# A two-layer block on one core: the first loads on two queues, the first LayerNorm in pairs of tiles, one weight product moved to the second batch, GpSimd's splits moved to VectorE, and W2's preparation tied to gates

## The chip, the cores and the metric

The kernel runs on one core of a Trainium2 chip. Its time is device time in microseconds, from runs of the whole program; the median of three runs is the number that counts. The profile is one execution of the same program, read by the hardware profiler, and its times are counted from the first instruction (the span's start).

## The reference

The input is x of shape (4, 512, 256): four batches of 512 tokens with 256 features. Two layers are applied. Because the state of the first layer's recurrence starts at zero and only one step is taken, the recurrence is a product with one fixed matrix. With `ln` for LayerNorm without scale, and `H` for the Walsh-Hadamard transform over 1024 values:

```
layer 0:  n  = ln(x)
          s  = n + rmsnorm(n @ M) * norm_w        M = W_in.T * diag(g) * W_out.T
layer 0 gate:  x = x + s * silu(ffn(n))           ffn(n) = H(silu(n @ W1.T) * (n @ W3.T)) @ W2.T
layer 1:  n  = ln(x)
          s  = n + causal_attention(ln(n) * gamma + beta)
layer 1 gate:  x = x + s * silu(ffn(n))           with the second layer's W1, W2, W3
output x
```

In the kernel the attention's query and key weights are multiplied once to one matrix (wqk), and its value and output weights to another (wvo). H is symmetric, so the kernel applies it to W2 once, and not to the hidden values. All values are float32; the kernel splits each operand into a high and a low part of 12 bits (hi + lo), so that a float32 product is three passes of TensorE: hi*hi, hi*lo, lo*hi.

## The kernel before

**Phases.** The work is eight phases in a row: four batches in layer 0, then four in layer 1. The body of a phase is one feed-forward block, `ffn` (L310), of a whole batch. It goes over eight chunks of 128 hidden values. For each chunk TensorE computes two banks of up products (`f_0gu` for batch 0 of layer 0: one bank with W1, one with W3; 6 products of 512 columns each, L70). ScalarE takes silu of the first bank (L363), VectorE multiplies it with the second (L364, the gate product), and `split` (L59) makes hi and lo: a copy on ScalarE (L61) and a subtraction (L62). Then TensorE adds the chunk's down products (`f_0dn`, L332). The banks `gu` are three, so every third bank waits for the silu or the gate product that frees it.

**Beside.** All other work (LayerNorm, mixer, attention, weight preparation) is written as generators. `Beside` spreads their steps over the 16 slots of a feed-forward block. A scheduler of the language then decides the order of each engine's queue; `tc.issue_after` (through `after`, L307) forces one instruction behind another.

**The first phase.** Batch 0 of layer 0 is special, for the weights must be prepared in it. `ffn` gets `parts=2` (chunk 0 in two halves of the tokens), `NH` as `defer` (all down products stay until the end), and `behind=True`, which puts the slots behind the gate products. In front of it stands the start:

- SP issues all loads, in the order: four tiles of x, the identity, qk, W13's part 0, vo, W13's part 1, the two halves of W2, the Hadamard matrix, bc, W_out, W_in, W13's parts 2 and 3, and small ones.
- Seven products of zeros (`warm`, L582) keep TensorE busy while the loads are under way.
- `norm_first` (L263) takes each of the four token tiles on its own: statistics and sum on VectorE, the power on GpSimd (L238), normalisation on VectorE (L240), two transposes on TensorE (L273), and the split of the transposed tile into `xth` (ScalarE) and `xtl` (VectorE).
- `prep_qk` computes wqk from the query and key weights, `prep_vo` computes wvo, and three butterfly stages of W2's first half (L125, L126) follow.
- `split_w13` (L97) splits W13's four parts, each 128x1024, when `ffn` first needs them. Parts 2 and 3 of layer 0 have their subtraction on GpSimd:

```python
engine = nc.gpsimd if layer == 0 and q >= 2 else nc.vector
```

- `prep_w2` (L113) transforms W2 by three butterfly stages on VectorE and a product with the Hadamard matrix on TensorE (`w2ps`; the first half in float32, the second in two passes after a split).
- `prep_m` (L178) makes M: a few small VectorE operations, four scalings on ScalarE (`wg`), and a product on TensorE (`mps`).

Of the kernel before, what the change touches and what calls it, by code (L numbers as in the profile page):

```python
# [21 lines left out]
P = 128  # L22
D = 256
# [12 lines left out]
def kernel(ctx: ExitStack, tc: tile.TileContext, a: dict, out: bass.AP):  # L36
# [22 lines left out]
    def split(src, hi, lo, engine=nc.vector):  # L59
        """hi + lo = src, exactly."""  # L60
        nc.scalar.copy(hi, src)  # L61
        engine.tensor_tensor(lo, src, hi.bitcast(F32), ALU.subtract)  # L62

    def mm3(o, terms):
        """o = sum over terms of lhs.T @ rhs, each operand a pair (hi, lo)."""
        seq = [(l[0], r[0]) for l, r in terms]
        for l, r in terms:
            seq += [(l[0], r[1]), (l[1], r[0])]
        for n, (l, r) in enumerate(seq):
            nc.tensor.matmul(o, l, r, start=n == 0, stop=n == len(seq) - 1)  # L70

# [6 lines left out]
    def load_x(b, nt=NT):  # L78
        xs[b] = x_slot(f"x{b}", [P, NT, D])
        src = a["x"][b].rearrange("(t p) d -> p t d", p=P)  # L80
        for t in range(0, NT, nt):
            nc.sync.dma_start(xs[b][:, t : t + nt, :], src[:, t : t + nt, :])
# [9 lines left out]
    def load_w13(layer, q):  # L92
        raw = t4(f"w13raw_{layer}_{q}", [P, 2, S])
        nc.sync.dma_start(raw, a[f"w13_{layer}"][q])
        return raw

    def split_w13(layer, q, raw):  # L97
        hi = wp.tile([P, 2, S], F32R, tag="w13h", name=f"w13h_{layer}_{q}", bufs=4)
        lo = wp.tile([P, 2, S], F32R, tag="w13l", name=f"w13l_{layer}_{q}", bufs=4)
        for c in range(2) if (layer, q) == (0, 0) else (slice(None),):  # L100
            cs = slice(c * D, (c + 1) * D) if c in (0, 1) else c
            engine = nc.gpsimd if layer == 0 and q >= 2 else nc.vector
            split(raw[:, :, cs], hi[:, :, cs], lo[:, :, cs], engine)
# [9 lines left out]
    def prep_w2(layer, raws, dst, scratch):  # L113
        """Rows of W2 under the Walsh-Hadamard transform (it is symmetric, so it may act on
        W2 in place of the hidden values): over the 8 blocks by butterflies, over the 128
        rows of a block by a product with the +-1/32 matrix."""
        w2h, w2l = dst
        for half in range(2):
# [10 lines left out]
            # in float32 it costs TensorE two passes more, but no split beforehand  # L129
# [23 lines left out]
    def product_of_weights(name, lhsT, rhs, nk, scale=None):  # L153
        """[256, 256] = lhsT.T @ rhs over nk chunks of 128, in float32, as a (hi, lo) pair."""
        hi = wp.tile([P, 2, D], F32R, name=f"{name}h")
        lo = wp.tile([P, 2, D], F32R, name=f"{name}l")
        o = psum(f"{name}ps", [P, 2, D])
        for i in range(2):
# [19 lines left out]
    def prep_m(win, wout):  # L178
        """xi*(sum of C_real*B_real - C_imag*B_imag) between W_in and W_out is one matrix."""
# [16 lines left out]
    def load_pair(name):  # L196
        raw = t4(f"{name}raw", [P, 2, 2, D])
        nc.sync.dma_start(raw, a[name])
        return raw

    def prep_qk(qk):
        return product_of_weights(
            "wqk", lambda k, i: qk[:, 0, k, sl(i)], lambda k: qk[:, 1, k, :], 2, 1.0 / 16.0
        )
# [7 lines left out]
    def moments(name, x, mr):  # L212
        """mr[:, 0] = the tokens' means, mr[:, 1] = their 1 / sqrt(variance + eps)"""
# [10 lines left out]
    def layernorm(name, x, y, groups=(NT,)):  # L224
        """y = layernorm(x), the token tiles in groups of these sizes"""
# [37 lines left out]
    def norm_first():  # L263
        """norm(0, 0), each token tile on its own"""
# [4 lines left out]
        layernorm("ln0_0", xs[0], xn, (1,) * NT)  # L269
        for t in range(NT):  # L270
            o = psum(f"xt0_0tp{t}", [P, 2, P])
            for k in range(2):
                nc.tensor.transpose(o[:, k, :], xn[:, t, sl(k)], ident)  # L273
            split(o, hi[:, :, sl(t)], lo[:, :, sl(t)])

    def norm(layer, b):
# [4 lines left out]
        layernorm(f"ln{layer}_{b}", xs[b], xn)  # L281
        yield
        if layer:
            # The second normalisation acts on the transposed values: its moments as rows of
            # all tokens, in every partition.
# [24 lines left out]
    def ffn(name, xT, w13, w2, slot, defer=1, spare=(), last=None, parts=1, behind=False):  # L310
        """Up, silu gate, down with the transformed W2: two PSUM banks of two token tiles.
        The down products of a chunk follow the up products of the defer-th after it.
        spare: pairs of tiles that hold the split hidden values of the first chunks.
        last: called with each token tile's result, finished one after the other, each in a
        bank of its own."""
# [20 lines left out]
                    # A start clears the accumulate bits of its whole bank: the bank's second  # L336
                    # tile begins without one, behind the first's.
# [10 lines left out]
        for c in range(NH):  # L348
# [7 lines left out]
            for half in range(parts if c == 0 else 1):  # L356
                n = S // (parts if c == 0 else 1)
                ts_ = slice(half * n, (half + 1) * n)
                for o, cols in gu:
                    mm3(o[:, ts_], k_pairs((wh, wl), cols, xT, ts_))  # L360
# [3 lines left out]
            gates.append(nc.vector.tensor_tensor(h, h, gu[1], ALU.mult))  # L364
            if c < len(spare):
# [6 lines left out]
            with after(gates[-1] if behind else None):  # L372
# [386 lines left out]
```

## Time and profile before

| what | value |
|---|---|
| runs | 372.45, 373.54, 375.09 us; median 373.54 us |
| profiled execution | span 370.9 us, 5491 instructions; no other time of it is given |
| TensorE (PE) busy | 361.5 us, 97% of the span |
| VectorE (DVE) busy | 248.0 us, 67% |
| ScalarE (ACT) busy | 179.7 us, 48% |
| GpSimd (POOL) busy | 36.2 us, 10% |
| loads and stores | 15.50 MB in 8969 packets |
| chain that ended last | PE 90%, DVE 5%, DMA 2% |

How to read it: a row of the profile names the line of the kernel, the engine, the operation, and what is written from what is read by the program's own names with buffer numbers left out, so `f_0gu` stands for both banks of all eight chunks in the first layer's first batch (and the second layer's). A busy share is of the whole span. In the slices each digit is the busy share of 1/40 of the span in tenths. "Idle before" names the instruction or load that ended an engine's idle time.

### The profile page before, as it was taken

The page shows a single profiled execution, that of the slowest core. Times are in us where ns is not written, and L with a number is a line of the kernel's source. Part 1 is how long each engine was busy: PE and PEld are TensorE (multiplying, and loading weights), DVE is VectorE, ACT ScalarE, POOL GpSimd, SP SyncE. Part 2 cuts the span into 40 slices and gives each one's busy share as a digit, 9 for nine tenths or more (in the row PEclk, how much of TensorE's full clock was granted, in tenths as well). Part 3 has the DMA queues.
Part 4 walks back from the last instruction along what each step waited for, and adds up shares of the span by engine and source line. Part 5 has one row for each costly group of instructions (what it writes and reads, how often), then busy time and mean ns, then how long its engine had stood idle before and what let it go on. Part 6 is the DMA issues. An engine that isn't in the chain of part 4 may idle for free.

```text
span 370.9 us, 5491 instructions
## 1 busy us (share of the span) xinstructions
PE 361.5 (97%) x2167; PEld 318.2 (86%) x2167; DVE 248.0 (67%) x519; ACT 179.7 (48%) x334; POOL 36.2 (10%) x30
## 2 busy tenths in 40 slices
PE   6997999999999999999999999999999999999995
PEld 4875999888888898889888998988989898888895
DVE  6898948996499339945949487465846447374644
ACT  2765334624453335445553654266633646356451
POOL 2060023410025002400011000010000000000000
PEclk9999999999999999999999999999999999999999
DMA  7915200000000040110010001100003000010001
GB/s 234 389 51 203 80 2 1 2 0 2 0 3 0 0 171 0 58 57 2 1 59 0 0 2 57 59 1 2 0 2 114 2 0 1 2 57 2 1 2 57
DMA packets 8969, 15.50 MB, mean 42 GB/s; under 512 B 848, under 2 KB 6640, under 8 KB 8944
## 3 DMA queue, kind: packets, MB, share of 16 engines
q1 hardware_dynamic: 8944, 15.16, 11.7%
q8 instruction: 17, 0.28, 0.3%
q14 instruction: 8, 0.07, 0.1%
HBM read 13.04 MB, written 2.11 MB: 41 GB/s over the span
## 4 chain that ended last, share of the span: by engine, by line
PE 90%; DVE 5%; DMA 2%; SPq 1%; issue 0%; ACT 0%; DVEq 0%
PE f_3gu L70 12%; PE f_2gu L70 12%; PE f_1gu L70 12%; PE f_0gu L70 8%; PE f_0dn L332 6%; PE f_3dn L332 6%; PE f_1dn L332 6%; PE f_2dn L332 6%; PE sc L70 4%; PE pv L70 4%; PE o L70 3%; PE v L70 3%; PE tq L70 3%; DMA w2raw<-in_w 2%; DVE w2b L125 1%; PE pt L498 1%
## 5 line engine op out<-in xcount | busy, mean ns | idle before, releaser
L70 PE MATMUL f_0gu<-xtl,w13h 128*128 128x512 f32 (+1 forms) x68 | 25.8, 382 | 0.0
L70 PE MATMUL f_1gu<-xth,w13l 128*128 128x512 f32 x64 | 25.5, 399 | 0.0
L70 PE MATMUL f_0gu<-xth,w13l 128*128 128x512 f32 (+1 forms) x68 | 25.5, 384 | 0.0
L70 PE MATMUL f_3gu<-xtl,w13h 128*128 128x512 f32 x64 | 25.5, 398 | 0.0
L70 PE MATMUL f_2gu<-xth,w13l 128*128 128x512 f32 x64 | 25.3, 396 | 0.0
L70 PE MATMUL f_3gu<-xth,w13l 128*128 128x512 f32 x64 | 25.3, 396 | 0.0
L70 PE MATMUL f_1gu<-xtl,w13h 128*128 128x512 f32 x64 | 25.3, 396 | 0.0
L70 PE MATMUL f_2gu<-xtl,w13h 128*128 128x512 f32 x64 | 25.3, 395 | 0.0
L70 PE MATMUL f_0gu<-xth,w13h 128*128 128x512 f32 (+1 forms) x68 | 21.3, 393 | 2.5 <-DVE f_0h L364 2.5
L364 DVE TENSOR_TENSOR f_2h<-f_2h,f_2gu 128x512 f32<-128x512 f32 x16 | 10.9, 681 | 19.1 <-PE f_2gu L70 11.0
L61 ACT CAST f_2hh<-f_2h 128x512 fp32r<-128x512 f32 x16 | 9.9, 621 | 23.0 <-DVE f_2h L364 23.0
L70 PE MATMUL f_2gu<-xth,w13h 128*128 128x512 f32 x64 | 20.7, 397 | 0.0
L70 PE MATMUL f_1gu<-xth,w13h 128*128 128x512 f32 x64 | 20.7, 398 | 0.0
L70 PE MATMUL f_3gu<-xth,w13h 128*128 128x512 f32 x64 | 20.6, 397 | 0.0
L61 ACT CAST f_3hh<-f_3h 128x512 fp32r<-128x512 f32 x16 | 9.9, 620 | 19.7 <-DVE f_3h L364 19.7
L332 PE MATMUL f_3dn<-w2l,f_3hh 128*128 128x256 f32 x64 | 17.6, 281 | 0.0
L332 PE MATMUL f_2dn<-w2l,f_2hh 128*128 128x256 f32 x64 | 17.6, 282 | 0.0
L332 PE MATMUL f_3dn<-w2h,f_3hh 128*128 128x256 f32 x64 | 17.5, 281 | 0.0
L332 PE MATMUL f_2dn<-w2h,f_2hh 128*128 128x256 f32 x64 | 17.5, 281 | 0.0
L332 PE MATMUL f_1dn<-w2l,f_1hh 128*128 128x256 f32 x64 | 17.4, 281 | 0.0
L332 PE MATMUL f_1dn<-w2h,f_1hh 128*128 128x256 f32 x64 | 17.3, 281 | 0.0
L363 ACT ACTIVATE f_2h<-f_2gu 128x512 f32<-128x512 f32 x16 | 9.5, 596 | 16.0 <-PE f_2gu L70 16.0
(227 smaller groups left out, 1104.4 us busy)
## 6 DMA issues: line engine op xcount, KB each, us to landing
w13raw<-in_w SPq DMA_DIRECT2D x8, 512.0 KB, 6.2
w2raw<-in_w SPq DMA_DIRECT2D x4, 512.0 KB, 6.8
mrb<-there SPq DMA_DIRECT2D x4, 512.0 KB, 3.7
x<-in_x SPq DMA_DIRECT2D x3, 512.0 KB, 3.7
out<-x SPq DMA_DIRECT2D x6, 256.0 KB, 2.1
x<-in_x SPq DMA_DIRECT2D x4, 128.0 KB, 2.2
qkraw<-in_qk SPq DMA_DIRECT2D x1, 512.0 KB, 4.7
voraw<-in_vo SPq DMA_DIRECT2D x1, 512.0 KB
```

What stands on the lines that cost most here:

```text
L61: nc.scalar.copy(hi, src)
L70: nc.tensor.matmul(o, l, r, start=n == 0, stop=n == len(seq) - 1)
L125: nc.vector.tensor_tensor(nv[:, :, 0], cv[:, :, 0], cv[:, :, 1], ALU.add)
L332: return nc.tensor.matmul(o, l[:, sl(t)], r[:, c, :], start=start, stop=stop, skip_group_check=True)
L363: nc.scalar.activation(h, gu[0], AF.Silu)
L364: gates.append(nc.vector.tensor_tensor(h, h, gu[1], ALU.mult))
L498: nc.tensor.transpose(pt[:, sl(j)], p[:, sl(j)], ident)
```

## The change

- **Loads.** x's four tiles go out by SP and ScalarE in turns, and qk follows on ScalarE's queue. On SP come the identity, W13's part 0 in two halves, part 1, W2, the Hadamard matrix, parts 2 and 3, and then bc, W_out and W_in. vo is no longer loaded at the start.
- **First LayerNorm.** `norm_first` is a generator: two pairs of tiles, each with one sum and one power, four transposes into one bank, and one split of 512 columns. The product of qk is cut in two (`product_qk`); its first half stands ahead of the first pair's transposes, its second half behind them.
- **Order.** `split_w13` puts the second half of part 0 behind the splits of the transposed x, and later parts behind that. Chunk 0's products go by term (hi*hi of both banks, then hi*lo, then lo*hi). A slot stands behind the gate product and behind the chunk's last up product. LayerNorms of batches 2 and 3 stand behind a gate product.
- **Weights.** W2's preparation runs in the slots, with no step of it in the start; the split of wqk and the load of the next x follow it. wvo is made in the second batch.
- **GpSimd** has no part in the splits of W13 any more.
- There are eight products of zeros instead of seven.

```diff
-            nc.sync.dma_start(xs[b][:, t : t + nt, :], src[:, t : t + nt, :])
+            queue = queues[t // nt % len(queues)]
+            queue.dma_start(xs[b][:, t : t + nt, :], src[:, t : t + nt, :])
...
     def load_w13(layer, q):
         raw = t4(f"w13raw_{layer}_{q}", [P, 2, S])
-        nc.sync.dma_start(raw, a[f"w13_{layer}"][q])
+        n = 2 if (layer, q) == (0, 0) else 1
+        for cs in (slice(i * S // n, (i + 1) * S // n) for i in range(n)):
+            nc.sync.dma_start(raw[:, :, cs], a[f"w13_{layer}"][q][:, :, cs])
...
     def split_w13(layer, q, raw):
...
-        for c in range(2) if (layer, q) == (0, 0) else (slice(None),):
-            cs = slice(c * D, (c + 1) * D) if c in (0, 1) else c
-            engine = nc.gpsimd if layer == 0 and q >= 2 else nc.vector
-            split(raw[:, :, cs], hi[:, :, cs], lo[:, :, cs], engine)
+        if (layer, q) != (0, 0):
+            split(raw, hi, lo)
+            return hi, lo
+        halves = [slice(c * D, (c + 1) * D) for c in range(2)]
+        split(*(z[:, :, halves[0]] for z in (raw, hi, lo)))
+        next(normed)
+        with after(first["norm"][0]), after(first["norm"][1]):
+            hi_, lo_ = split(*(z[:, :, halves[1]] for z in (raw, hi, lo)))
+        first["w13"] = hi_, lo_
...
+    def product_qk(qk):
+        o = psum("wqkps", [P, 2, D], tag="dn", bufs=2)
+        for i in range(2):
+            for k in range(2):
+                ins = nc.tensor.matmul(
+                    o[:, i, :], qk[:, 0, k, sl(i)], qk[:, 1, k, :], start=k == 0, stop=k == 1
+                )
+            yield o, ins
...
-    def norm_first():
+    def norm_first(qk):
...
-        layernorm("ln0_0", xs[0], xn, (1,) * NT)
-        for t in range(NT):
-            o = psum(f"xt0_0tp{t}", [P, 2, P])
-            for k in range(2):
-                nc.tensor.transpose(o[:, k, :], xn[:, t, sl(k)], ident)
-            split(o, hi[:, :, sl(t)], lo[:, :, sl(t)])
+        x = xs[0]
+        ins, pairs = None, []
+        for i in range(2):
...
+            with after(ins):
+                for t in (2 * i, 2 * i + 1):
+                    nc.vector.bn_stats(st[:, t, :], x[:, t, :])
+                for t in (2 * i, 2 * i + 1):
+                    nc.vector.bn_aggr(mv[:, t, :], st[:, t, :])
+                rs = r[:, 2 * i : 2 * i + 2]
+                ins = nc.vector.tensor_scalar(
+                    rs, mv[:, 2 * i : 2 * i + 2, 1], LN_EPS, None, ALU.add
+                )
+            nc.gpsimd.tensor_tensor(rs, rs, mhalf[:, :2], ALU.pow)
+            pairs.append((mv, r))
+        for i, (mv, r) in enumerate(pairs):
+            for t in (2 * i, 2 * i + 1):
+                with after(ins):
+                    ins = nc.vector.tensor_scalar(
+                        xn[:, t, :], x[:, t, :], mv[:, t, 0:1], r[:, t : t + 1], ALU.subtract, ALU.mult
+                    )
+        products = product_qk(qk)
+        first["wqkps"], ins = next(products)
+        yield
+        hi_ = lo_ = None
+        for i in range(2):
+            ts_ = slice(2 * i * P, 2 * (i + 1) * P)
+            o = psum(f"xt0_0tp{i}", [P, 2, 2 * P])
+            with after(ins):
+                for t in (2 * i, 2 * i + 1):
+                    for k in range(2):
+                        ins = nc.tensor.transpose(o[:, k, sl(t - 2 * i)], xn[:, t, sl(k)], ident)
+            with after(hi_):
+                hi_ = nc.scalar.copy(hi[:, :, ts_], o)
+            with after(lo_):
+                lo_ = nc.vector.tensor_tensor(
+                    lo[:, :, ts_], o, hi[:, :, ts_].bitcast(F32), ALU.subtract
+                )
+            if i == 0:
+                with after(ins):
+                    _, ins = next(products)
+        first["norm"] = hi_, lo_
+        yield
...
     def norm(layer, b):
...
-        layernorm(f"ln{layer}_{b}", xs[b], xn)
+        with after(first["gate"] if layer == 0 and b > 1 else None):
+            layernorm(f"ln{layer}_{b}", xs[b], xn)
...
     def ffn(name, xT, w13, w2, slot, defer=1, spare=(), last=None, parts=1, behind=False):
...
-                for o, cols in gu:
-                    mm3(o[:, ts_], k_pairs((wh, wl), cols, xT, ts_))
+                if parts == 1 or c:
+                    for o, cols in gu:
+                        last_up = mm3(o[:, ts_], k_pairs((wh, wl), cols, xT, ts_))
+                    continue
+                for n, (w, x) in enumerate(((wh, xT[0]), (wl, xT[0]), (wh, xT[1]))):
+                    for o, cols in gu:
+                        for k in range(2):
+                            last_up = nc.tensor.matmul(
+                                o[:, ts_], w[:, k, cols], x[:, k, ts_],
+                                start=n + k == 0, stop=n + k == 3,
+                            )
...
+            first["gate"] = gates[-1]
...
-            with after(gates[-1] if behind else None):
+            ups = last_up if behind else None
+            with after(gates[-1] if behind else None), after(ups):
                 slot(2 * c)
...
-    load_x(0, 1)
+    load_x(0, 1, (nc.sync, nc.scalar))
+    qk = load_pair("qk", nc.scalar)
...
-    for i in range(7):
+    for i in range(8):
         nc.tensor.matmul(warm, zr[:, :P], zr, start=True, stop=True)
     nc.sync.dma_start(ident, a["ident"])
-    qk = load_pair("qk")
-    raw13 = [load_w13(0, 0)]
-    vo = load_pair("vo")
-    raw13 += [load_w13(0, 1)]
+    raw13 = [load_w13(0, q) for q in range(2)]
     raw2 = load_w2(0)
     nc.sync.dma_start(had_f, a["hadamard"])
+    raw13 += [load_w13(0, q) for q in range(2, 4)]
     raw_m = load_m()
-    raw13 += [load_w13(0, q) for q in range(2, 4)]
...
-    norm_first()
+    normed = norm_first(qk)
+    next(normed)
...
     def w13(q):
-        if q not in w13_0:
+        if q == 0 and not w13_0:
             w13_0[q] = split_w13(0, q, raw13[q])
+        elif q not in w13_0:
+            with after(first["w13"][0]), after(first["w13"][1]):
+                w13_0[q] = split_w13(0, q, raw13[q])
...
     def prep_first():
-        first["wqk"] = prep_qk(qk)
+        steps = prep_w2(0, raw2, w2, x_slot)
+        for _ in range(5):
+            next(steps)
+            yield
         nc.scalar.copy(had, had_f)
+        yield from steps
+        with after(first["w13"][0]):
+            first["wqk"] = product_of_weights("wqk", None, None, 2, 1.0 / 16.0, first["wqkps"])
         yield
-        steps = prep_w2(0, raw2, w2, x_slot)
-        for _ in range(3):
-            next(steps)
-        yield
-        first["wvo"] = prep_vo(vo)
-        yield
-        yield from steps
         load_x(1)
         first["m"] = prep_m(*raw_m)
         yield
+    def prep_second():
+        first["wvo"] = prep_vo(load_pair("vo"))
+        yield
...
             prep = prep_first()
-            for _ in range(3):
-                next(prep)
-            tasks.append((prep, 10))
+            tasks.append((prep, 13))
...
             tasks.append((prep_w2(1, raw2_1, w2_1, t4), W2P))
+            tasks.append((prep_second(), 1))
```

More of the change, by code (lines that the diff above doesn't have):

```diff
@@ L59, in split @@
     def split(src, hi, lo, engine=nc.vector):
-        nc.scalar.copy(hi, src)
-        engine.tensor_tensor(lo, src, hi.bitcast(F32), ALU.subtract)
+        h = nc.scalar.copy(hi, src)
+        return h, engine.tensor_tensor(lo, src, hi.bitcast(F32), ALU.subtract)
     def mm3(o, terms):
@@ L69, in mm3 @@
         for n, (l, r) in enumerate(seq):
-            nc.tensor.matmul(o, l, r, start=n == 0, stop=n == len(seq) - 1)
+            ins = nc.tensor.matmul(o, l, r, start=n == 0, stop=n == len(seq) - 1)
+        return ins
     xs = {}
@@ L76, in x_slot, with load_x @@
         return wp.tile(shape, F32, tag="x", name=name, bufs=B)
-    def load_x(b, nt=NT):
+    def load_x(b, nt=NT, queues=(nc.sync,)):
         xs[b] = x_slot(f"x{b}", [P, NT, D])
@@ L151, in w2_tiles, with product_of_weights @@
         return w2_tile(f"w2h_{layer}"), w2_tile(f"w2l_{layer}")
-    def product_of_weights(name, lhsT, rhs, nk, scale=None):
+    def product_of_weights(name, lhsT, rhs, nk, scale=None, o=None):
         hi = wp.tile([P, 2, D], F32R, name=f"{name}h")
         lo = wp.tile([P, 2, D], F32R, name=f"{name}l")
-        o = psum(f"{name}ps", [P, 2, D])
-        for i in range(2):
+        for i in range(2) if o is None else ():
+            o = o if i else psum(f"{name}ps", [P, 2, D])
             for k in range(nk):
@@ L194, in sl, with load_pair @@
         return slice(i * P, (i + 1) * P)
-    def load_pair(name):
+    def load_pair(name, queue=nc.sync):
         raw = t4(f"{name}raw", [P, 2, 2, D])
-        nc.sync.dma_start(raw, a[name])
+        queue.dma_start(raw, a[name])
         return raw
[L201 to L204, printed above, removed]
+    def product_qk(qk):
[6 more added lines that the diff above has]
+            yield o, ins
     def prep_vo(vo):
@@ L268, in norm_first @@
         xns[0, 0], xTs[0, 0] = xn, (hi, lo)
-        layernorm("ln0_0", xs[0], xn, (1,) * NT)
-        for t in range(NT):
-            o = psum(f"xt0_0tp{t}", [P, 2, P])
-            for k in range(2):
-                nc.tensor.transpose(o[:, k, :], xn[:, t, sl(k)], ident)
-            split(o, hi[:, :, sl(t)], lo[:, :, sl(t)])
+        x = xs[0]
+        ins, pairs = None, []
+        for i in range(2):
+            st = act.tile([P, NT, 6], F32, tag="stats", name=f"ln0_0st{i}", bufs=4)
+            mv = act.tile([P, NT, 2], F32, tag="mv", name=f"ln0_0mv{i}", bufs=4)
+            r = small(f"ln0_0r{i}")
+            with after(ins):
[37 more added lines that the diff above has]
+        yield
     def norm(layer, b):
@@ L375, in ffn @@
                 down(*queue.pop(0))
-            with after(gates[-1] if behind else None):
+            with after(gates[-1] if behind else None), after(ups):
                 slot(2 * c + 1)
@@ L594 @@
     nc.sync.dma_start(mask, a["mask"])
-    norm_first()
+    first = {}
+    normed = norm_first(qk)
+    next(normed)
     w13_0 = {}
     def w13(q):
-        if q not in w13_0:
+        if q == 0 and not w13_0:
             w13_0[q] = split_w13(0, q, raw13[q])
+        elif q not in w13_0:
+            with after(first["w13"][0]), after(first["w13"][1]):
+                w13_0[q] = split_w13(0, q, raw13[q])
         return w13_0[q]
@@ L604 @@
     w2 = w2_tiles(0)
-    first = {}
     def prep_first():
-        first["wqk"] = prep_qk(qk)
+        steps = prep_w2(0, raw2, w2, x_slot)
+        for _ in range(5):
+            next(steps)
+            yield
         nc.scalar.copy(had, had_f)
+        yield from steps
+        with after(first["w13"][0]):
+            first["wqk"] = product_of_weights("wqk", None, None, 2, 1.0 / 16.0, first["wqkps"])
         yield
-        steps = prep_w2(0, raw2, w2, x_slot)
-        for _ in range(3):
-            next(steps)
-        yield
-        first["wvo"] = prep_vo(vo)
-        yield
-        yield from steps
         load_x(1)
         first["m"] = prep_m(*raw_m)
+        yield
+    def prep_second():
+        first["wvo"] = prep_vo(load_pair("vo"))
         yield
```

## The prediction

> **What bounds the kernel now.** I read the page's slices first, then TensorE's waits, then the timelines of the first 32 us. In the slices each column is 9.27 us.
>
> ```profile
> PE   6997999999999999999999999999999999999995
> PEclk9999999999999999999999999999999999999999
> GB/s 234 389 51 203 80 2 1 2 0 2 0 3 0 0 171 0 58 57 2 1 59 0 0 2 57 59 1 2 0 2 114 2 0 1 2 57 2 1 2 57
> ```
>
> TensorE is busy almost throughout, at full clock; only the first and fourth columns have room. The engine's waits are few (engine, line, whom it waited for: us, times, longest):
>
> ```profile
> PE f_0gu L70 <- DVE f_0h L364: 2.5, 1, 2.5
> PE xt_0tp L273 <- DVE ln_0r L237: 0.5, 1, 0.5
> ```
>
> So the change can win in two places only: the start, and this one stall. Everything it moves later must fit under TensorE, or be TensorE work moved whole. The windows of the stretches (length, then busy time per engine):
>
> ```profile
> 5.79:9.78 3.99, 3.47 (x17) 2.33 (x17) 2.25 (x8) 1.74 (x5) 1.05 (x3) 1.00 1.01 407
> 28.53:31.43 2.90, 0.40 (x3) 0.01 (x1) 2.90 (x6) 0.56 (x1) 0.00 (x0) 1.00 0.60 184
> ```
>
> In the second row VectorE is busy for all of it and TensorE for 0.40. VectorE's and TensorE's timelines say why (start, us, instruction):
>
> ```profile
> 21.45 0.68 DVE L364 TENSOR_TENSOR f_0h<-f_0h,f_0gu 128x512 f32<-128x512 f32 x1
> 22.04 2.32 DVE L62 TENSOR_TENSOR early<-f_0h,early 128x512 fp32r<-128x512 f32 x1
> 24.29 2.88 DVE L125 TENSOR_TENSOR w2b<-w2b 128x512 f32<-128x512 f32 x1
> 27.09 0.68 DVE L126 TENSOR_TENSOR w2b<-w2b 128x512 f32<-128x512 f32 x1
> 30.70 1.27 DVE L364 TENSOR_TENSOR f_0h<-f_0h,f_0gu 128x512 f32<-128x512 f32 x2
> ```
>
> ```profile
> 31.43 0.73 PE L70 MATMUL f_0gu<-xth,w13h 128*128 128x512 f32 x2 [2.50 <-DVE f_0h L364]
> ```
>
> ```profile
> L62 POOL TENSOR_TENSOR w13l<-w13raw,w13h x2: 2870/3186/3503, 20.3 to 23.8; 128x1024 fp32r<-128x1024 f32 x2
> ```
>
> Two VectorE operations that take 0.68 elsewhere take 2.32 and 2.88 while GpSimd splits W13. The gate products at 30.70 stand behind them, and TensorE waits for a bank that they free.
>
> **Start, part by part.** The changed program's order on each engine is fixed when it is built, and I follow it. ScalarE's timeline and the loads (times from issue to landing) of before:
>
> ```profile
> 11.69 1.05 ACT L61 CAST w13h<-w13raw 128x1024 fp32r<-128x1024 f32 x1 [0.67 <-DMA w13raw<-in_w]
> 13.74 1.28 ACT L363 ACT_TABLE_LOAD   x1
> 15.03 0.60 ACT L363 ACTIVATE f_0h<-f_0gu 128x512 f32<-128x512 f32 x1
> ```
>
> ```profile
> qkraw<-in_qk SPq DMA_DIRECT2D x1, 512.0 KB, 4.7
> x<-in_x SPq DMA_DIRECT2D x4, 128.0 KB, 2.2
> ```
>
> Loads. SP issues one each 0.45 us (four of x in 1.80). On two queues x is issued by 1.6 instead of 2.5, and qk, third on ScalarE's queue, at 1.63 instead of 3.06. ScalarE's first table load (1.28) moves behind three issues, to some 2.0 to 3.3; its first copy comes after 5, so this costs nothing. With 4.7 us to landing, qk is there at 6.4 (before: 7.8). [...] No trace of before shows two issuing queues. [...] Below, 5.5 is possible, as x itself comes sooner. I take 6.4: the 4.7 us already held a wait behind x and ident.
>
> LayerNorm. Four statistics (0.43), four aggregates (0.17) and two sums are the same as before; GpSimd's powers are two instead of four (0.55 each). From x at 2.9, all statistics end by 5.4 and the four normalisations (0.33 apart) by 6.9. This is hidden, for the first transposes stand in TensorE's queue behind the first half of qk's product: with qk at 6.4, four records of 0.216 end at 7.3, four transposes (some 0.5) at 7.8, the second half at 8.7, the other transposes at 9.15. The first f_0gu product starts at 9.15 instead of 9.78: **-0.63 us**. The eighth product of zeros (0.43) ends before 5.6, ahead of qk, and costs nothing; with qk earlier than that it would cost its overlap.
>
> vo. Its product (8 records of 0.216, 1.73 us) leaves the start and returns between batches 1 and 2. It is TensorE work in both: nothing gained. Its load waits on SP for a buffer, and later issues stand behind it, first the row exchange of the second LayerNorm, at 128 us in before; the buffer is free some 50 us earlier. Nothing.
>
> First gate. What the pins add is on ScalarE and VectorE. ScalarE's order is now: second xth copy (0.51 apart), W13's second half (0.51), w13h of part 1 (0.95), wqkh (0.51), had (0.2), table load (1.28), first silu (0.60). From 9.4 that ends at 13.97. TensorE has done the 24 half-width products of chunk 0 (24 x 0.117) by 11.95 and the first bank of chunk 1 (6 x 0.234) by 13.35; the next bank is chunk 0's, freed by that silu: **+0.6**. VectorE sat free until 13.98, as W2's butterflies are gated behind the first gate product. Then come gate, two butterflies and w13l of part 1 (0.6 + 1.2 + 1.22 = 3.0): ready at 17.0. TensorE starts chunk 2 at 15.4 and needs it after six products, at 16.8: **+0.26**.
>
> **GpSimd's splits.** The two stretched operations return 1.6 and 2.2 us to VectorE; the two splits cost it 2 x 1.14 instead (the 128x1024 one at 16.70 has its follower at 17.84). LayerNorm statistics of batches 2 and 3 (eight at 0.33, eight aggregates at 0.08, 3.3 us) also leave this stretch, later under slack. VectorE runs without a break from the first gate: up to the fifth gate product 20 operations of 512 columns at 0.60 and two of 1024 at 1.14, 14.3 us, so this gate starts at 28.26 and ends at 28.9 (before: 31.30). TensorE comes there at 28.6: chunks 2 to 5 (4 x 2.81), the two float32 products of W2 (1.73) and the 0.26, from 15.4. The stall of 2.66 (28.77 to 31.43) goes, **-2.66**, and 0.4 stays, **+0.40**.
>
> **What is late next.** VectorE's queue now sets four smaller waits. The copy of the fifth hidden chunk (0.51) and the silu behind it (0.61) free the next bank at 30.15, TensorE is there at 29.7: +0.46. wqkl, w13l of part 3 and the last butterflies end at 31.9, ScalarE's copy of them (1.05) at 33.0, TensorE is there at 32.26: +0.76. The W_out scaling stands on ScalarE behind the last silu, which waits for the last up products at 37.0; 0.6 + 0.5 later M's product can start, with TensorE there since 37.2: +1.2. At the next block's first bank +0.3. Together **+2.7**. I hold these at 0 to 4, as the order at TensorE is fixed and each is a difference of two queues.
>
> **Sum.** -0.63 + 0.6 + 0.26 - 2.66 + 0.40 + 2.7 = +0.7 us. After 60 us the two programs have the same products and VectorE has slack, so it stays to the end. On the profiled span of 370.9 this gives 371.6. The median of the runs, 373.54, lies 2.6 above that span; what lies around a span (start and end of an execution) is untouched, so I add 0.7 to the median: **374.2**. A measurement of this kernel can tell about 1% (3.7 us) from no change, and the runs before spread by 0.7%; this is "no change". (The page gives no time of the profiled execution beyond its span.)
>
> **Rivals.** (A) The waits of the VectorE queue don't appear, because the copies and gates overlap more than I lined them up: -0.63 - 2.66 plus half of the 4.0 of new stalls is -1.3 (372.2), and with qk at 5.5 and only 1 us of new stalls -3.2 (370.3). For it: before, VectorE recovers from its stretch by itself at 38. Against: it works without a break for over 20 us, and each gate stands in its order. (B) Slower: qk comes late. The first half of its product stands ahead of all transposes, the transposes ahead of the first silu and all gates, so one us later is one us on the end. W13's first part, issued at 3.53, landed at 9.1 in before; were qk to share its fate and come at 9.5, the sum is +0.7 + 3.1 = +3.8 (377.3). It decides from 9.4 on. W13's part 1 later than about 9 costs in the same way. [...] Against: only 1.1 MB of x, ident and qk are needed, 2.8 us at 389 GB/s, from 1.8. (C) The pins don't do what they say and the start is unchanged: then only GpSimd's part counts, -1 to 0 (373.0).
>
> **Numbers.** Forecast 0.60; A 0.19, of which 0.07 beyond 1%; B 0.14, of which 0.11 beyond 1%; C 0.07. Faster 0.07, within 1% 0.82, slower 0.11. The range runs from A's middle with the spread of the runs, 372.0, to B, 377.0.
>
> **What would show it.** Right: f_0gu first at about 9.2; no VectorE operation over 1.3 us before 40; the 2.5 us wait replaced by several under 1.3; the first silu at 13.4. Wrong: qk landing after 8; TensorE waiting over 1.5 us in one place before 60; a new wait after 60.

## The result and the profile after

The changed kernel takes 376.0 us (median of 11 runs, 374.29 to 377.36), the kernel before 373.41 us on the same chips (11 runs, 372.30 to 375.65). The ratio is 1.0066, with a 95% interval from 1.0043 to 1.0089: slower by 0.7%, within the 1% that was called no change, and inside the range. The sign was right, the size was not: +2.5 us where +0.7 was forecast. The profiled execution has a span of 373.2 us and took 374.97 us, so some 1.8 us lie around a span.

The slices after, where one column is 9.33 us:

```profile
PE   7999999999999999999999999999999999999995
PEclk9999999999999999999999999999999999999999
GB/s 269 343 2 113 169 3 0 7 51 2 0 2 1 0 2 169 58 56 2 58 3 0 0 2 56 58 1 2 0 2 113 0 2 1 2 56 2 0 3 56
```

The hole in the fourth column is gone, and the profile looks better than before: TensorE is 98% busy instead of 97%. But a TensorE that runs at half its clock is also busy (in the run a_nopin, below, for all 3.00 us from 9 to 12, at a granted clock of 0.51). The waits after (us in total, times, longest) are the small ones that were forecast, and one for qk:

```profile
PE mps L171 <- ACT wg L199: 0.9, 1, 0.9
PE f_0gu L70 <- ACT f_0h L430: 0.7, 2, 0.5
PE wqkps L217 <- DMA qkraw<-in_qk: 0.6, 1, 0.6
PE w2ps L152 <- ACT w2bh L61: 0.5, 1, 0.5
PE f_0gu L70 <- DVE f_0h L431: 0.2, 1, 0.2
```

For sums I use the starts of TensorE's products: whatever a product's successor starts later than the full-clock pace of its kind (0.234 us for 512 columns of a split operand, 0.216 for a qk record) is lost time. Apart from the zeros both programs have the same 2160 products, some 356 us at this pace, so three numbers explain a span: when the first `f_0gu` product starts, what is lost from there to 60 us, and what is lost later.

| execution | first f_0gu | lost to 60 us | lost later | span |
|---|---|---|---|---|
| before | 9.78 | 2.99 | 0.73 | 370.9 |
| after | 10.80 | 4.30 | 0.78 | 373.2 |
| difference | +1.02 | +1.31 | +0.05 | +2.3 |
| forecast | -0.63 | +1.30 | 0 | +0.7 |

In sum the middle came out as forecast (in part by luck, as the part on the prediction shows). The start did not, and all of the miss in this execution is there. TensorE's timeline of after's start (start, us, instruction, then idle time before it and its releaser):

```profile
4.63 1.05 PE L653 MATMUL warm<-zr 128*128 128x512 f32 x2
6.27 2.07 PE L217 MATMUL wqkps<-qkraw 128*128 128x256 f32 x4 [0.58 <-DMA qkraw<-in_qk]
8.13 1.06 PE L319 MATMUL xt_0tp<-ident,xn 128*128 128x128 f32 x4
8.99 1.62 PE L217 MATMUL wqkps<-qkraw 128*128 128x256 f32 x4
10.45 0.60 PE L319 MATMUL xt_0tp<-ident,xn 128*128 128x128 f32 x4
```

qk is there at 6.23, even a little before the 6.4 of the forecast. But its first four records need from 6.27 to 8.13, not 0.9 us. In before the pace was twice as fast:

```profile
8.01 1.99 PE L160 MATMUL wqkps<-qkraw 128*128 128x256 f32 x8
9.78 0.39 PE L70 MATMUL f_0gu<-xth,w13h 128*128 128x256 f32 x1
```

Eight records in 1.77 us in before, eight in 3.3 us in after. In the trace's clock records TensorE is granted the full clock at 6.27 us in before and at 10.18 us in after; in after the qk records are 0.427 us apart until then, twice the 0.216. The windows view hides it (stretch, length, busy time of PE, PEld, DVE, ACT and POOL with instructions, granted clock, DMA share, GB/s):

```profile
6.00:9.00 3.00, 2.73 (x9) 2.27 (x10) 1.68 (x4) 0.62 (x1) 0.56 (x1) 1.00 1.04 381
```

The clock column says 1.00, since no clock record precedes the first grant. What tells is the count: the nine products in these 2.73 us (five qk records, four transposes) would take 1.5 at the full-clock paces of 0.216 and 0.109 us.

The loads (KB, us from issue to landing) are as forecast for qk in this one execution, while x gained nothing from its two queues: a tile needed 2.2 in before, and VectorE's first statistics start at 3.23 instead of 2.90:

```profile
qkraw<-in_qk ACTq DMA_DIRECT2D x1, 512.0 KB, 4.6
...
x<-in_x SPq DMA_DIRECT2D x2, 128.0 KB, 2.5
x<-in_x ACTq DMA_DIRECT2D x2, 128.0 KB, 3.0
```

ScalarE's first silu, forecast for 13.4, starts at 15.13:

```profile
13.84 1.28 ACT L430 ACT_TABLE_LOAD   x1
15.13 0.60 ACT L430 ACTIVATE f_0h<-f_0gu 128x512 f32<-128x512 f32 x1
```

### The profile page after: what moved, and what is told of

The parts are those of the page before. It is cut to its first block, busy times and chain, and to the rows that moved or that the text cites. A ratio compares the mean times of both kernels' runs of the same rounds, so it can differ in the third digit from the quotient of the medians.

```text
span 373.2 us, 5474 instructions
## 1 busy us (share of the span) xinstructions
PE 364.5 (98%) x2168; PEld 320.1 (86%) x2168; DVE 243.7 (65%) x517; ACT 179.9 (48%) x332; POOL 30.7 (8%) x26
## 3 DMA queue, kind: packets, MB, share of 16 engines
HBM read 13.04 MB, written 2.11 MB: 41 GB/s over the span
## 4 chain that ended last, share of the span: by engine, by line
PE 89%; DVE 5%; ACT 2%; DMA 1%; issue 1%; ACTq 0%
PE f_2gu L70 12%; PE f_3gu L70 12%; PE f_1gu L70 12%; PE f_2dn L389 6%; PE f_3dn L389 6%; PE f_1dn L389 6%; PE f_0dn L389 6%; PE f_0gu L70 6%; PE sc L70 4%; PE pv L70 4%; PE v L70 3%; PE o L70 3%; PE tq L70 3%; DMA qkraw<-in_qk 1%; PE pt L567 1%; DVE f_0h L431 1%
## 5 line engine op out<-in xcount | busy, mean ns | idle before, releaser
L70 PE MATMUL f_0gu<-xtl,w13h 128*128 128x512 f32 x60 | 23.7, 395 | 0.0
L70 PE MATMUL f_0gu<-xth,w13l 128*128 128x512 f32 x60 | 23.4, 401 | 0.0
L70 PE MATMUL f_0gu<-xth,w13h 128*128 128x512 f32 x60 | 19.1, 400 | 0.9 <-ACT f_0h L430 0.7
L61 ACT CAST f_1hh<-f_1h 128x512 fp32r<-128x512 f32 x16 | 9.9, 620 | 18.6 <-DVE f_1h L431 18.6
```

Of the source, the lines that this page charges most:

```text
L61: h = nc.scalar.copy(hi, src)
L70: ins = nc.tensor.matmul(o, l, r, start=n == 0, stop=n == len(seq) - 1)
```

## The experiments

Each is one edit of before or of after. Differences between kernels are differences of their ratios to the runs of before that went beside them, times 373.4 us.

| kernel | edit | median us (runs) | ratio to before | first f_0gu | lost to 60 | lost later |
|---|---|---|---|---|---|---|
| before_again | before, another execution | 372.06 (1) | | 9.48 | 2.67 | 0.73 |
| after_again | after, another execution | 376.44 (1) | | 11.95 | 4.41 | 0.77 |
| b_dve | before, no splits on GpSimd | 370.95 (6) | 0.9930 [0.9903, 0.9957] | 9.56 | 1.05 | 0.64 |
| a_gps | after, splits on GpSimd again | 380.83 (4) | 1.0184 [1.0146, 1.0222] | 11.85 | 9.12 | 0.84 |
| a_nopin | after, first W2 steps unpinned | 374.49 (22) | 1.0023 [1.0007, 1.0039] | 12.74 | 1.75 | 1.60 |
| a_warm12 | after, 12 products of zeros | 376.06 (8) | 1.0065 [1.0039, 1.0090] | 10.46 | 3.01 | 4.46 |
| a_np_qksp | a_nopin, qk by SP | 373.94 (14) | 1.0007 [0.9986, 1.0028] | 11.36 | 1.75 | 1.60 |
| a_np_tp | a_nopin, qk's product behind the transposes | 373.02 (22) | 0.9986 [0.9971, 1.0000] | 11.36 | 1.04 | 1.60 |
| a_fill | a_np_tp, more zeros | 371.71 (6) | 0.9933 [0.9909, 0.9958] | 10.09 | 1.96 | 0.77 |
| b_dve_x2 | b_dve, x by two queues | 371.87 (19) | 0.9952 [0.9936, 0.9968] | 11.54 | 1.04 | 0.68 |
| b_dve_vo | b_dve, vo in batch two | 371.81 (16) | 0.9953 [0.9935, 0.9971] | 11.48 | 1.09 | 0.77 |
| b_fill | b_dve, more zeros | 370.43 (6) | 0.9912 [0.9886, 0.9937] | 11.81 | 0.36 | 0.73 |

The last three columns are of one execution each. The start varies between executions of one kernel; the middle varied by 0.1 (after) and 0.3 us (before).

### GpSimd's part by itself: b_dve and a_gps

b_dve does only this part of the change, in the kernel before:

```diff
-            engine = nc.gpsimd if layer == 0 and q >= 2 else nc.vector
+            engine = nc.vector
```

> The kernel before with one edit: the subtractions of W13's parts 2 and 3 on VectorE instead of GpSimd. Theory (the stall of 2.66 us came from the stretch beside GpSimd): the stall at 28.5 us goes, what is left later in the first phase is about 0.7, and the time falls by 1.5 to 2 us against the kernel before, to about 371.7. Rival (VectorE's queue becomes the bound, 2.3 us more work on it): the stall moves and stays above 2 us, the time is within 0.5 us of the kernel before.

a_gps takes only this part back, in the kernel after:

```diff
-            split(raw, hi, lo)
+            split(raw, hi, lo, nc.gpsimd if layer == 0 and q >= 2 else nc.vector)
```

> The changed kernel with the subtractions of W13's parts 2 and 3 back on GpSimd. Theory (shared stretch): VectorE operations beside them are stretched again to 2 to 3 us, TensorE waits more than 1.5 us in one place between 15 and 30 us, and the time is 1 to 2 us longer than the changed kernel's, about 377.5. Rival (VectorE is relieved of 2.3 us of work, which is worth more than the stretch): the time is 0.5 to 1.5 us shorter.

b_dve is 2.6 us faster than before: what is lost to 60 us falls from 2.99 to 1.05, since the one stall of 2.67 goes and a wait of 0.60 at 33.5 stays. So this part of the forecast holds, and the rest of the change costs some 5 us (376.0 against 370.95, on different chips; by the ratios 5.1).

a_gps lost 4.4 us against after, not 1 to 2. Its waits, and VectorE's timeline with GpSimd's two splits (durations in ns, shortest, median, longest; then the starts):

```profile
PE f_0gu L70 <- DVE w13l L62: 4.3, 1, 4.3
```

```profile
18.13 2.90 DVE L136 TENSOR_TENSOR w2b<-w2raw 128x512 f32<-128x512 f32 x1
20.95 3.36 DVE L62 TENSOR_TENSOR w13l<-w13raw,w13h 128x1024 fp32r<-128x1024 f32 x1
```

```profile
L62 POOL TENSOR_TENSOR w13l<-w13raw,w13h x2: 2571/2676/2782, 17.9 to 20.4; 128x1024 fp32r<-128x1024 f32 x2
```

A butterfly of 0.69 takes 2.90 and the split of part 1, 1.22 in after, takes 3.36 while GpSimd works. In before the stretched operations had only butterflies and a gate behind them. Here W2's pins have pushed part 1's split, which TensorE needs at once, into the same stretch. And during the wait, which lasted from 20.0 to 24.36, the granted clock fell, which was not expected:

```profile
12.00:60.00 48.00, 42.27 (x223) 35.32 (x223) 32.69 (x54) 22.77 (x42) 6.33 (x3) 0.93 0.30 102
```

The granted clock (the third number from the end) is 0.93 over these 48 us: it was half from 22.43 to 29.26.

### W2's pins: a_nopin

The first three butterfly steps of W2's first half run before the feed-forward block, as in before, instead of behind the first gate products:

```diff
             prep = prep_first()
-            tasks.append((prep, 13))
+            for _ in range(3):
+                next(prep)
+            tasks.append((prep, 10))
```

> The changed kernel with the three butterfly stages of W2's first half taken out of the gated slots and put ahead of the feed-forward block, as in the kernel before; all else is the changed kernel's. Theory (pins): VectorE sat free from about 13 to 15.8 us with the butterflies pinned behind the first gate, and the four waits of TensorE after 28 us (0.34 + 0.35 + 0.66 + 1.04) and the one at 18 us are what it owes; they should shrink to one below 0.7, and the time fall by 2.0 to 2.6 us, to about 373.6. Rival (VectorE's total work is the bound, wherever it stands): the waits stay above 2 us in sum and the time falls by less than 0.7 us.

What is lost to 60 us fell from 4.30 to 1.75, by 2.55, and 0.8 us came back as a wait at 78.0: VectorE's small operation of 0.17 us (`ln_2r`, L253) took 2.38 at 75.84, beside an addition of 3.33 us on GpSimd. The time fell by 1.6 us. So VectorE's late queue, the +2.7 of the forecast, is real, though smaller, and it is the pins that make it. Before them VectorE stands idle with butterflies at hand:

```profile
12.31 0.68 DVE L62 TENSOR_TENSOR w13l<-w13raw,w13h 128x512 fp32r<-128x512 f32 x1
15.77 0.69 DVE L431 TENSOR_TENSOR f_0h<-f_0h,f_0gu 128x512 f32<-128x512 f32 x1 [2.77 <-ACT f_0h L430]
16.37 0.68 DVE L135 TENSOR_TENSOR w2b<-w2raw 128x512 f32<-128x512 f32 x1
```

This is VectorE in after: 2.77 us of idleness, and then without a break to 36. The start of a_nopin was the worst of all, though its start was not edited:

```profile
8.44 1.50 PE L217 MATMUL wqkps<-qkraw 128*128 128x256 f32 x4 [2.74 <-DMA qkraw<-in_qk]
9.73 1.06 PE L319 MATMUL xt_0tp<-ident,xn 128*128 128x128 f32 x4
10.59 1.91 PE L217 MATMUL wqkps<-qkraw 128*128 128x256 f32 x4
12.29 0.69 PE L319 MATMUL xt_0tp<-ident,xn 128*128 128x128 f32 x4
```

```profile
9.00:12.00 3.00, 3.00 (x11) 2.43 (x10) 1.25 (x2) 1.13 (x2) 0.00 (x0) 0.51 1.04 410
```

qk landed at 8.39, 2.2 us later than in after with the same loads in the same order, and the clock, granted at 5.64, was half again from 9.05 to 12.47.

### Two more executions: after_again and before_again

No edit; one more profile of each kernel, for how much of a start is chance.

> The changed kernel as it is, for a second execution's profile. Theory (the landing of qk differs from execution to execution): qk lands at 7 us or later instead of 6.23, f_0gu begins at 11 to 12.7 instead of 10.80 (with the clock at full or not), the idle of TensorE between f_0gu and 60 us is again 4.3, and the span lies 0.5 to 2 us above 373.2. Rival (the late qk of the other kernels comes from their edits): qk lands within 0.3 us of 6.23 and f_0gu begins within 0.3 of 10.80.

> The kernel before as it is, for a second execution's profile. Theory (the clock's windows lie differently in each execution): its span differs from 370.9 by up to 2 us, through the start alone; the clock is granted at a moment other than 6.27 us, qk lands at 7.3 to 8.1, and the stall of 2.7 us near 28 to 31 us is there again. Rival (the start is the same in each): f_0gu begins within 0.2 us of 9.78.

In the middle after_again repeats after: the first wait is 0.44 instead of 0.69 us, and the others are the same at the same products (0.16, 0.34, 0.35, 0.66 and 1.04). In the start it doesn't: qk landed at 7.98 instead of 6.23, the clock was granted at 5.90, then half from 9.31 to 12.73, and the first `f_0gu` product starts at 11.95.

In before_again qk landed at 7.20 and the start was at 9.48. In both kernels the middle changes by 0.1 to 0.3 us only, so the 1.0 us by which after's profiled run lay below its median is likely its early qk; two profiles don't prove it.

### The clock: a_warm12

> The changed kernel with twelve products of zeros in place of eight, so that TensorE has no gap between them and the product of qk (landed at 6.23 us). Theory (cold clock): the changed kernel lost its start because the clock was granted only at 10.18 us, so that the qk product ran at 0.427 us a record instead of 0.216. Without a gap the clock should be granted by about 6 to 9 us, f_0gu should begin at 8.8 to 9.8 instead of 10.80, and the time fall by 1.0 to 1.3 us (not by the whole 2, since the load of the Hadamard matrix, landed at 12.49, stands ahead of the first silu on ScalarE): about 374.8. Rival (the clock's grant falls by chance and the gap has no part in it): the time stays within 0.5 us of the changed kernel, or is up to 0.9 us longer, as the four products delay qk's.

```diff
-    for i in range(8):
+    for i in range(12):
```

The clock part came as expected: granted at 7.45, and nothing was lost between qk's arrival (7.79) and the first `f_0gu` product at 10.46. The time did not move (376.06). The extra zeros gave another order later on, in which a butterfly in the second batch stands beside an addition of GpSimd:

```profile
70.63 2.89 DVE L135 TENSOR_TENSOR w2b<-w2raw 128x512 f32<-128x512 f32 x1
69.66 3.32 POOL L494 TENSOR_TENSOR xn<-xn,osb 128x1024 f32<-128x1024 f32 x1 [3.35 <-DVE ln_2mv L251]
```

The butterfly takes 2.89 us instead of 0.68, TensorE waits 1.82 us for what VectorE does after it, and then has half clock for 3.4 us:

```profile
75.70:79.10 3.40, 3.40 (x12) 2.81 (x11) 3.40 (x7) 1.44 (x3) 2.21 (x1) 0.50 0.00 0
```

So an operation of VectorE can still take four times as long beside one of GpSimd when the splits are gone. As a test of what the clock is worth in time this run is spoilt.

### The order at TensorE and qk's queue: a_np_tp and a_np_qksp

a_np_tp keeps a_nopin's loads but puts both halves of qk's product behind all transposes, as before had them:

```diff
-        products = product_qk(qk)
-        first["wqkps"], ins = next(products)
+        ins = None
         yield
...
-            if i == 0:
-                with after(ins):
-                    _, ins = next(products)
+        products = product_qk(qk)
+        for _ in range(2):
+            with after(ins):
+                first["wqkps"], ins = next(products)
```

> a_nopin's kernel with the two halves of qk's product behind all transposes on TensorE, qk still on ScalarE's queue. Theory (order): a late qk then holds up nothing on the way to the first silu; the transposes begin at about 6.4 us, f_0gu at 8.5 to 10.5, and the time falls against a_nopin by 0.5 to 1.5 us, to about 373.5, even where qk lands at 8. Rival (the first silu is set by the loads of W13 and the Hadamard matrix anyway): f_0gu begins earlier but the waits before chunk 1 grow by as much, and the time stays within 0.4 us of 374.5.

a_np_qksp keeps a_nopin's order but issues qk on SP, behind the identity:

```diff
     load_x(0, 1, (nc.sync, nc.scalar))
-    qk = load_pair("qk", nc.scalar)
...
     nc.sync.dma_start(ident, a["ident"])
+    qk = load_pair("qk")
     raw13 = [load_w13(0, q) for q in range(2)]
```

> The changed kernel with W2's first butterflies ahead of the block (as in a_nopin), and with qk's load moved from ScalarE's queue to SP's, between the identity and W13. x stays on two queues. Theory (interleaving): qk's 4 KB packets were held up on some of the 16 engines by W13's half-loads on the other queue, so that qk landed at 6.2 to 8.4 us from execution to execution; in one queue it comes first and lands at 6.0 to 6.8, W13's first half about 7.5 to 8.3. Then TensorE's wait for qk falls from 2.7 us to under 1, and the time falls against a_nopin by 0.7 to 1.5 us, to about 373.3. Rival (the memory side is slow at the start whatever the queue): qk still lands at 7.5 or later and the time stays within 0.4 us of a_nopin's 374.5.

The order is worth 1.4 us (0.9986 against 1.0023), of which 0.7 is in the middle (1.75 to 1.04), though the first `f_0gu` product starts at 11.36 in its profile and not by 10.5 as expected. With qk first, everything up to the first `f_0gu` product stands behind its arrival, 2.7 us at full clock (a_warm12); with the transposes first only qk's eight records do, 1.8 us (a_fill). The queue is worth some 0.6 us, and the intervals overlap, so it is not shown: qk issued at 2.11 on SP landed at 7.21 (6.0 to 6.8 was expected), while issued at 1.66 on ScalarE in a_nopin it landed at 8.39.

TensorE waits 1.6 us for the load of a_np_qksp and 2.74 for the one of a_nopin, its parent, which was issued earlier. In a_nopin's trace 260 of qk's 512 KB had come by 5.5 us, in after's 472, though W13's first half-loads (packets of 1 KB on SP's queue) had by then moved only 7 KB in the one and 2 KB in the other. So qk was late before they came. What was left then came slowly beside them: per half microsecond qk's packets (4 KB) fall from 96 KB at 5.5 to 24 KB at 7.5, while those of 1 KB reach 117 KB at 6.5. Why qk was slow in one execution and not in the other stays open.

### Order and clock together: a_fill

a_np_tp with the clock kept: ten products of zeros instead of eight, and two of 256 columns behind each pair's transposes.

```diff
+            with after(ins):
+                for j in range(2):
+                    ins = nc.tensor.matmul(warm[:, :256], zr[:, :P], zr[:, :256], start=True, stop=True)
...
-    warm = psum("warm", [P, S])
-    for i in range(8):
+    warm = psum("warm", [P, S], tag="dn", bufs=2)
+    for i in range(10):
```

> a_np_tp with TensorE kept busy through the start: ten products of zeros instead of eight, and two half-width ones behind each pair of transposes. The scheduler also puts the later vo and W2 work in another order, in which no wait over 0.5 us is left after chunk 1. [...]

371.71 us, 2.0 us faster than a_np_tp by the ratios, and its six runs lie within 0.6 us (21 of a_np_tp's 22 within 1.1). qk landed at 8.29, later than in a_np_tp (7.06), and yet the first `f_0gu` product starts at 10.09 instead of 11.36:

```profile
8.33 1.99 PE L217 MATMUL wqkps<-qkraw 128*128 128x256 f32 x8
10.09 0.74 PE L427 MATMUL f_0gu<-xth,w13h 128*128 128x256 f32 x4
```

In a_np_tp the same eight records took from 8.46 to 11.36, since the clock was granted only at 11.21. The clock is kept, but in this execution most of the 1.27 us is lost again. ScalarE now comes to the Hadamard matrix before it has landed (13.69), and the first silu behind it starts at 15.32, against 14.32 in a_np_tp:

```profile
13.71 0.30 ACT L687 CAST had<-had_f 128x128 fp32r<-128x128 f32 x1 [1.22 <-DMA had_f<-in_hadamard]
```

TensorE waits 1.57 us for it at the second bank of chunk 1. The zeros also changed the scheduler's order: the waits at 33.6 and 75.9 are gone. The table's differences to a_np_tp are -1.27 in the start, +0.92 to 60 us and -0.83 later. How much of the 2.0 us between the medians is the clock's is therefore not shown.

### The rest of the change, and zeros for before: b_dve_x2, b_dve_vo, b_fill

All three stand on b_dve. x's tiles 1 and 3 by ScalarE:

```diff
-            nc.sync.dma_start(xs[b][:, t : t + nt, :], src[:, t : t + nt, :])
+            queue = nc.scalar if nt == 1 and t % 2 else nc.sync
+            queue.dma_start(xs[b][:, t : t + nt, :], src[:, t : t + nt, :])
```

> b_dve (the kernel before, W13's splits on VectorE) with one more edit: the second and fourth tile of x issued by ScalarE. Theory (issuers share engines): x's last tile lands within 0.3 us of b_dve's 4.5, f_0gu begins within 0.4 us of 9.6, and the time stays within 0.5 us of b_dve's 371.0. Rival (a second queue brings x sooner): x lands at 3.5 and f_0gu begins 0.5 us or more earlier, the time falls by 0.5 us or more.

vo's load and product in batch two:

```diff
-    vo = load_pair("vo")
...
-        first["wvo"] = prep_vo(vo)
...
+    def prep_second():
+        first["wvo"] = prep_vo(load_pair("vo"))
+        yield
...
+            tasks.append((prep_second(), 1))
```

> b_dve with one more edit: vo's load and product moved to the second batch, as in the changed kernel. Theory (filler): vo's product filled TensorE while the first silu was awaited; without it TensorE waits 1 to 2.5 us before chunk 1's second bank, less what the earlier loads give (W13's part 1 lands about 1.3 us earlier, at 9.9), and the product is paid again later: 0.5 to 2 us slower than b_dve, about 372.3. Rival (moved work costs nothing, my prediction's own step): the time stays within 0.4 us of b_dve's 371.0, or falls with the earlier loads.

One product of zeros behind each tile's transposes:

```diff
-    warm = psum("warm", [P, S])
+    warm = psum("warm", [P, S], tag="dn", bufs=2)
...
+            with after(ins):
+                for i in range(1):
+                    nc.tensor.matmul(warm[:, :256], zr[:, :P], zr[:, :256], start=True, stop=True)
```

> b_dve with one half-width product of zeros behind each token tile's two transposes, so that TensorE is not idle for long between 5.6 and 8 us. Theory (clock): executions in which the clock came only at about 11.6 us (as in b_dve_x2 and b_dve_vo) get it by 9 us, and the median falls by 0.3 to 1 us below b_dve's 371.0. Rival: the extra products delay the transposes or the wait before chunk 1 takes the gain, and the time stays within 0.3 us or rises.

Two queues gained nothing: the tile that ScalarE issued at 0.74 landed at 3.61 and the one that SP issued at 1.19 at 4.06, while in b_dve, on one queue, the first, issued at 0.74, landed at 2.86 and the third, issued only at 1.64, at 3.83. The time is 0.8 us above b_dve's by the ratios, with intervals that overlap. vo moved is inconclusive: also 0.9 us above, but the wait that was expected before chunk 1's second bank isn't there (1.09 us lost to 60 us, 1.05 in b_dve). In both, the profiled execution had half clock from 8.2 to 11.6, which moved the first `f_0gu` product to 11.5 and hides what the edits do.

b_fill has the lowest median of all, 370.43 us: 0.9912 to before, and so 1.5% ahead of after. Against b_dve (0.9930) the intervals overlap. Its profile doesn't show the clock gained: the identity landed only at 6.78, and the clock came at 11.05.

Not tried by themselves were the LayerNorm in pairs, the order of chunk 0's products by term, the slots behind the last up product, and the LayerNorms of batches 2 and 3 behind a gate.

## Why the prediction was right or wrong

- **GpSimd's splits** were right: the 2.67 stall is gone, no VectorE operation takes more than 1.23 us before 40. -2.66 was forecast, and b_dve, which makes this change alone, gained 2.6 us.
- **First gate**: +0.6 forecast, 0.69 measured (at 14.86); +0.26 forecast, 0.16 measured (at 18.45). These times are the starts of the product ahead of a wait.
- **What is late next**: 0.46, 0.76, 1.2 and 0.3 were forecast; 0.35 (at 31.36), 0.66 (33.91), 1.04 (38.97) and nothing came. The 0.40 ahead of them was 0.34 (30.22). a_nopin shows that W2's pins cause them. Nothing new came after 60, as forecast. By the prediction's own figures two of these terms are smaller than it says: at M's product 38.1 less 37.2 is 0.9 and not 1.2, and 28.9 less 28.6 is 0.3 and not 0.40.
- **The middle in sum**: +1.31 where the terms give +1.30, but in part by luck. The six waits make 3.24 us; less the stall of 2.67 that is +0.57. Most of the rest is a cost that no term had: the second product after a wait starts 0.10 us later than the pace, six times in after and once in before (+0.5), and the down products at 38.75 and 38.97 are 0.10 late as well. So the waits were forecast 0.7 us too large, and what was left out made up for it.
- **Start** is the step that failed: -0.63 forecast, +1.02 in after's profile and +2.17 in after_again's (11.95 against 9.78). Two terms of it were wrong.
  - *Records of 0.216 us.* I took the pace of qk's records from before, where the clock had come before them. In after the four stretches from 6.27 took 1.86, 0.86, 1.46 and 0.35 us, 4.53 together, where the forecast had 2.75. These +1.78 less the 0.13 by which the first record started early are the miss of 1.65. a_fill, with the clock kept, has its eight records in 1.76 us, and a_warm12 needs 2.67 from qk's landing to the first `f_0gu` product.
  - *qk at 6.4.* It was so in one execution of the seven that issue the loads as after does: 6.23 in after, but 7.98 (after_again), 8.39 (a_nopin), 7.67 (a_gps), 7.79 (a_warm12), 7.06 (a_np_tp) and 8.29 (a_fill). The median of the seven is 7.79, 1.4 us later than I took; counted one for one, as the prediction counts it, that would have made the sum about +2.1 and the time 375.6 (an estimate). In after_again the miss is this (qk 1.58 us after 6.4) and the clock (3.97 us from landing to the first `f_0gu` product, instead of 2.75) together.
- **First silu** at 13.4: it came 1.7 us later, which is the late start and little else: the second xth copy, ahead of it on ScalarE, began at 11.08 instead of 9.4, and ScalarE worked without a break from there.
- **Rival B** had the right mechanism, that a late qk delays the end as its product stands ahead of all transposes; a_np_tp confirms it from the other side. It is not one for one: in after_again qk came 1.75 us later than in after and the span is 1.2 longer, as the clock had come by then (granted at 5.90, against 10.18 in after). But qk never came as late as the 9.4 from which it should have decided. A did not happen: the waits are there. C did not: the order was as read.

What is shown: the splits' gain (b_dve, a_gps), the pins' cost (a_nopin), the order's cost (a_np_tp). Taking back the pins, taking back the order and keeping the clock leads from 1.0066 over 1.0023 and 0.9986 to 0.9933, which is b_dve's 0.9930 again: together these edits undo all that the change costs beside the splits. For the last of them the cause is argued only, as a_fill's zeros changed the order too. What stays open: how the last microsecond between after's profiled run (374.97) and its median (376.0) divides between qk's arrival and the clock, how much of a_fill's gain is the clock's, what vo's move does, and whether b_fill gains on b_dve.

## What to carry to other kernels

Before a product is put ahead of other work because its data will come sooner, count what then stands behind those data: here 2.7 us instead of 1.8, so that qk had to come 0.9 us earlier than before only to break even. Don't let an engine that is late twenty microseconds on stand idle now: a pin that held butterflies behind the first gate left VectorE free for 2.8 us and then cost 2.5 us of waits. When zeros are added to keep a clock, look at what they do to the order later and at what the earlier start then runs into: a_warm12 lost its gain that way, and a_fill's profiled execution most of what its start had won. And take a duration at the clock that holds where the work will run, not where the trace has it: the spacing of the records tells (0.427 us for a qk record in after, 0.216 in before), the busy share doesn't.

## What the runs showed of the hardware

**The granted clock.** The first grant of the full clock came anywhere from 4.78 (b_dve_x2) to 11.21 us (a_np_tp), at 6.27 in before and at 10.18 in after; ahead of it after's qk records were 0.427 us apart, behind it 0.216. In some executions the clock was later half for a stretch. The longest wait of TensorE next to six such stretches, and for comparison before's longest behind its start:

| execution | TensorE's wait | ends at | clock |
|---|---|---|---|
| b_dve_x2 | 0.71 us | 5.81 | half from 8.2 to 11.6 |
| b_dve_vo | 1.49 us | 6.60 | half from 8.2 to 11.6 |
| after_again | 2.33 us | 8.03 | half from 9.31 to 12.73 |
| a_nopin | 2.74 us | 8.44 | half from 9.05 to 12.47 |
| a_gps | 4.34 us | 24.36 | half from 22.43 to 29.26 |
| a_warm12 | 1.82 us | 74.92 | half from 75.7 to 79.1 |
| before | 2.50 us | 31.43 | 1.00 from 12 to 60 |

The length of the wait alone doesn't tell: 0.71 us in b_dve_x2 and 1.82 in a_warm12 were followed by half clock, 2.50 in before were not. What decides when the clock comes and goes is not shown by these runs. In after's start the 8 zeros end 0.6 to 2.7 us before qk's product, and there are no transposes in between; in none of the five profiles with this start on TensorE (after, after_again, a_nopin, a_gps, a_np_qksp) did qk's product have the full clock throughout. With 12 zeros, which end 0.4 us before it (a_warm12), and with a_fill's zeros behind the transposes it had: the eight records took 1.76 us in a_fill.

**qk's arrival.** The same load in the same place of the same program landed 6.23 and 7.98 us into two executions. With before's single queue it landed between 7.20 and 8.04 in the five profiles that keep it. It was issued 1.4 us earlier in after (1.65 against 3.06), and yet the medians are the same: 7.79 of the seven, 7.75 of the five. From 2 to 4 us the busy share of the 16 DMA engines was 0.94 in before, with one queue (243 GB/s), and 0.95 in after, with two (287 GB/s).

**VectorE beside GpSimd.** Operations of 0.68 us took 2.32 to 2.90 while GpSimd worked on a 128x1024 tile (before, a_gps, a_warm12), and one of 0.17 us took 2.38 (a_nopin). b_dve (2.6 us faster than before) and a_gps (4.4 us slower than after) show what that costs when TensorE waits for the result.
